# Four value buffers in a fused cross-attention, self-attention and expert kernel

## The chip, the cores and the metric

The kernel runs on one core of a Trainium2 chip, as one launch. The metric is the device time of the launch in microseconds (us); lower is better. A core has five engines that matter here: TensorE (PE in the profile; PEld is its weight load), VectorE (DVE), ScalarE (ACT), GpSimd (POOL) and SyncE (SP), which issues nearly all transfers.

## The reference

A batch of 64 sequences of 32 tokens, 256 wide, passes through three layers, each behind a layer norm and added back. The first attends from each sequence to its own 257 rows of context (`ctx_512`, 128 wide), the second attends within each sequence, with rotated queries and keys, the third sends each token to two of eight experts. Cut to that:

```
x = x + xattn(layernorm(x), ctx_512)     # 16 heads of 64; softmax over 257 context rows
x = x + attn(layernorm(x))               # 4 heads of 64; softmax over the 32 tokens of the sequence
x = x + ffn(layernorm(x))                # top 2 of 8 experts, silu(a) * b, 512 hidden
```

All of it is in float32.

## The kernel before, in words

The 2048 tokens are 16 tiles `t` of 128 tokens, each with four sequences `b`. The main loop goes over the 64 sequences `n` (`t, b`), and each iteration works at several tiles at once. `cross_probs` (L351 to L384) makes the scores of sequence n+1 against its context `kvT` (L364), the softmax on DVE and ACT, and the transposed weights `prT`. `cross_mix` (L395) runs in the odd iterations only: for the pair n-1 and n it multiplies the weights with the context itself, `kvA`, the "values" of a sequence. `cross_queries` prepares the queries of the next pair of tiles. The rest of a tile is a generator, `rest`: `cross_output` (values projected into `ov`, L429; output projection, L437), a norm `xns`, `self_attention`, a norm `xr`, and `route`, which picks two experts for each token and scatters the token's row into the table `routed` in DRAM (L616). Three tiles are at different steps of `rest`: "near", "far" and "late". A table of words, `steps`, says in which order an iteration takes these parts.

In `self_attention` the projected `qkv` is rotated on DVE, its queries and keys are turned by PE and copied by ACT into `qkT` (L471), PE multiplies them (L483), the softmax goes to a block-diagonal tile `diag` (L508), PE applies it (L513), ACT copies the result to `oT` (L520), and PE projects that (L527). A store of the tile (L530) follows on SP's queue.

The loads of the main loop are issued by SP, through `load` (L106): in iteration n the values of sequence n+2 (`load_values`, four transfers of 128 KB), the keys of sequence n+4, and at the end of a tile four small rows `u`. A buffer of `kvA` can be refilled once PE has mixed with it.

The expert layer works in blocks of 128 table rows that go to one expert. Six "early" blocks are formed while the last two tiles are not finished, their work interleaved with the rest of these tiles by the words of `do` (x: turn the block's rows, a and b: the two halves of the first layer, c: the second layer and the scatter into the output); the "late" blocks follow. For each block SP gathers the rows (`xg`, L733), and loads weights into "lanes" (L695). `prepared` (L763 to L777) turns the rows on PE, and DVE makes from the row's last columns the token's weight in this block (`gates` L773, `gate` L775) and its output row (`to` L777). These are used only in `combined` (L835 to L842). What the late blocks are is planned by some forty DVE operations once the last tile is routed (`late_blocks`, L656 to L945); SP reads its numbers (`meta_late`) before it gathers.

The order of instructions on PE and SP is that of the program text (`tc.manual_schedule(engines={SP, mybir.EngineType.PE})`). On DVE, ACT and POOL the framework's scheduler sets it when the kernel is built, by its own estimate of when each instruction could run; `tc.keep_in_program_order(...)` keeps one instruction of these engines behind the ones written ahead of it. Every engine runs its own instructions in the order so set. A tile's memory comes from a pool by tag: tiles of one tag share `bufs` buffers in turn, two in the pool `wk` unless the tile says otherwise.

Of the kernel before, what the change touches and what calls it, by code (L numbers as in the profile page):

```python
# [9 lines left out]
FP = mybir.dt.float32  # L10
U32 = mybir.dt.uint32
AF = mybir.ActivationFunctionType
ALU = mybir.AluOpType
# [3 lines left out]
P = 128  # L17
# [5 lines left out]
KVD = 128  # L23
M = 257
MC = 8
# [4 lines left out]
NE = 8  # L30
# [26 lines left out]
def block_kernel(  # L57
# [24 lines left out]
    nc = tc.nc  # L82
# [22 lines left out]
    def load(dst, src):  # L105
        nc.sync.dma_start(out=dst, in_=src)  # L106
# [10 lines left out]
    def pool(name, bufs):  # L117
        return ctx.enter_context(tc.tile_pool(name=name, bufs=bufs))

    kvp = pool("kv", 2)  # L120
# [10 lines left out]

    def load_values(n):

        kvA = kvp.tile([P, MC, KVD], FP, tag="kvA", bufs=3, name=f"kvA{n}")
        for h in range(4):
            load(kvA[h * SEQ : (h + 1) * SEQ, :, :], ctx_a[:, n, :, :])
        values.append(kvA)
# [15 lines left out]
    for n in range(2):  # L153
        load_values(n)
# [27 lines left out]
    wk = pool("wk", 2)  # L182
# [25 lines left out]
    for e in range(NE):  # L208
        tag, bufs, n = (("y", 4, D), ("bxT", 2, D), ("xg", 5, RW))[(e > 3) + (e > 5)]
# [10 lines left out]
    def bank(shape):  # L220
        return view(a_bank(), shape)
# [17 lines left out]
    def transposed(dst, src, n):  # L239

        pt = bank([n, P])
        for k in range(n):
            nc.tensor.transpose(pt[:, k, :], src[:, k * P : (k + 1) * P], ident)
        nc.scalar.copy(dst, pt)  # L244
# [200 lines left out]
    def self_attention(t, xn):  # L445
        xaT = wk.tile([P, 2, P], FP, tag="xaT", name=f"xaT{t}")
        transposed(xaT, xn, 2)
        yield
        qkv = wk.tile([P, 3 * D], FP, tag="qkv", name=f"qkv{t}")
        for lo, hi in ((0, 512), (512, 768)):  # L450
            pq = bank([hi - lo])
            for k in range(2):
                nc.tensor.matmul(  # L453
                    pq, xaT[:, k, :], awqkv_sb[:, k, lo:hi], start=(k == 0), stop=(k == 1)
                )
            nc.vector.tensor_tensor(qkv[:, lo:hi], pq, abqkv_bc[:, lo:hi], ALU.add)
        yield

        heads = qkv[:, : 2 * D].rearrange("p (h d) -> p h d", d=HD)
        x1, x2 = heads[:, :, 32:48], heads[:, :, 48:64]  # L460
        cb, sb = cos.to_broadcast([P, 2 * AH, 16]), sin.to_broadcast([P, 2 * AH, 16])
        x1s = wk.tile([P, 2 * AH, 16], FP, tag="x1s", name=f"x1s{t}")
        x2s = wk.tile([P, 2 * AH, 16], FP, tag="x2s", name=f"x2s{t}")
        tc.keep_in_program_order(nc.vector.tensor_tensor(x1s, x1, sb, ALU.mult))
        nc.vector.tensor_tensor(x2s, x2, sb, ALU.mult)
        nc.vector.tensor_tensor(x1, x1, cb, ALU.mult)
        nc.vector.tensor_tensor(x2, x2, cb, ALU.mult)
        nc.vector.tensor_tensor(x1, x1, x2s, ALU.subtract)
        nc.vector.tensor_tensor(x2, x2, x1s, ALU.add)
        yield  # L470
        qkT = wk.tile([P, 4, P], FP, tag="qkT", name=f"qkT{t}")  # L471
        transposed(qkT, qkv, 4)
        yield


        sc = wk.tile([P, 2, 2, SEQ], FP, tag="sc", name=f"sc{t}")
        mx = sm.tile([P, 2, 2, 1], FP, tag="amx", name=f"amx{t}")
        for par in range(2):
            pss = bank([2, SEQ])
            r = par * HD  # L480
            for hh in range(2):
                for b in range(4):
                    nc.tensor.matmul(  # L483
                        pss[b * SEQ : (b + 1) * SEQ, hh, :],
                        qkT[r : r + HD, hh, b * SEQ : (b + 1) * SEQ],
                        qkT[r : r + HD, 2 + hh, b * SEQ : (b + 1) * SEQ],
                        start=True,
                        stop=True,
                    )
            nc.vector.tensor_reduce(mx[:, par, :, :], pss, AX.X, ALU.max)  # L490
            nc.vector.tensor_tensor(
                sc[:, par, :, :],
                pss,
                mx[:, par, :, :].to_broadcast([P, 2, SEQ]),
                ALU.subtract,
            )
        scf = sc.rearrange("p a h s -> p (a h) s")
        pr = wk.tile([P, AH, SEQ], FP, tag="apr", name=f"apr{t}")
        nc.scalar.activation(pr, scf, AF.Exp, bias=zero, scale=QK_SCALE)
        sums = sm.tile([P, AH, 1], FP, tag="asums", name=f"asums{t}")  # L500
        nc.vector.tensor_reduce(sums, pr, AX.X, ALU.add)
        inv = sm.tile([P, AH, 1], FP, tag="ainv", name=f"ainv{t}")
        nc.vector.reciprocal(inv, sums)
        nc.vector.tensor_tensor(pr, pr, inv.to_broadcast([P, AH, SEQ]), ALU.mult)
        dg = diag[t % 2]
        for b in range(4):
            r = slice(b * SEQ, (b + 1) * SEQ)
            nc.vector.transpose(dg[r, :, r], pr[r, :, :])  # L508
        yield
        pot = bank([2, P])  # L510
        for h in range(AH):
            par, hh = h % 2, h // 2
            nc.tensor.matmul(  # L513
                pot[par * HD : (par + 1) * HD, hh, :],
                qkv[:, 2 * D + h * HD : 2 * D + (h + 1) * HD],
                dg[:, par * 2 + hh, :],
                start=True,
                stop=True,
            )
        oT = wk.tile([P, 2, P], FP, tag="oT", name=f"oT{t}")  # L520
        nc.scalar.copy(oT, pot)
        yield
        xb = wk.tile([P, D], FP, tag="xb", name=f"axb{t}")
        nc.gpsimd.tensor_tensor(xb, xs[t], abo_bc, ALU.add)
        po = bank([D])
        for k in range(2):
            nc.tensor.matmul(po, oT[:, k, :], awo_sb[:, k, :], start=(k == 0), stop=(k == 1))  # L527
        nc.vector.tensor_tensor(xs[t], po, xb, ALU.add)
        if t < NT - 2:
            nc.sync.dma_start(out=out[t * P : (t + 1) * P, :], in_=xs[t])  # L530
# [103 lines left out]
    def rest(t, cT, lastT, ut):  # L634

        yield from cross_output(t, cT, lastT, ut)
        xn = normed(t, "s")
        yield
        yield from self_attention(t, xn)
        xr = wk.tile([P, RW], FP, tag="xr", name=f"xr{t}")  # L640
        normed(t, "r", xr[:, 0:D])
        yield
        yield from route(t, xr)
# [66 lines left out]
    class Blocks:  # L710
# [44 lines left out]
        def prepared(self, b):  # L755

            xg, xw = self.xgs.pop(b)

            xT = xp.tile([P, 4, 2, SEQ], FP, tag="bxT", bufs=2, name=f"bxT_{self.name}{b}")
            if b < self.quarters:  # L760
                pt = bank([2, P])
                for k in range(2):
                    nc.tensor.transpose(pt[:, k, :], xg[:, k:D:2], ident)  # L763
                nc.scalar.copy(
                    xT.rearrange("p c k i -> p k c i"), pt.rearrange("p k (c i) -> p k c i", c=4)
                )
            else:
                nc.vector.transpose(
                    xT, xg[:, :D].rearrange("p (c j k) -> p c k j", c=4, k=2)
                )  # L770
            self.xTs[b] = xT
            gates = xp.tile([P, NE], FP, tag="gates", name=f"gates_{self.name}{b}")
            nc.vector.tensor_tensor(gates, xw[:, :NE], self.mine[:, b, :], ALU.mult)  # L773
            one = slice(b, b + 1)
            nc.vector.tensor_reduce(self.gate[:, one], gates, AX.X, ALU.add)  # L775
            if self.valid is None:
                nc.vector.tensor_copy(self.to[:, one], xw[:, NE:])  # L777
            else:
                nc.vector.scalar_tensor_tensor(
                    self.to[:, one], xw[:, NE:], self.valid[:, one],  # L780
                    self.spare[:, one], ALU.mult, ALU.add,
                )
# [354 lines left out]
    for n, (t, b) in enumerate(seqs):  # L1137
# [22 lines left out]
        if n + 2 < len(seqs):  # L1160
            load_values(n + 2)
# [177 lines left out]
```

## Time and profile before

| | us |
|---|---|
| median of 3 runs | 755.09 |
| lowest and highest run | 754.23, 756.03 |
| profiled execution: its own time | 758.28 |
| profiled execution: span, first to last instruction | 756.4 |
| busy in the span: PE, PEld, DVE, ACT, POOL | 723.9, 613.2, 508.4, 393.8, 322.2 |

The profile is of one execution, and its times within the span are counted from the span's start. A timeline line gives start, duration, engine, source line, operation, output and inputs, and in brackets how long the engine was idle before it and what released it. A line of waits gives who waited for whom, the total in us, how often, and the longest. A line of the form `L106 SPq` is SP's queue issuing a transfer: its duration is the issue, not the transfer. The attention tiles take about 66 us for each pair of tiles; the last tile's main loop ends near 533 us, the early blocks run to about 590 us, the late ones to 747 us.

### The profile page before, as it was taken

Reading aid. Unit: us, or ns where it says so; the run is one execution under the profiler, and the core shown is the slowest. Engines: PE = TensorE matmul, PEld = TensorE weight load, DVE = VectorE, ACT = ScalarE, POOL = GpSimd, SP = SyncE. Lnnn points to the kernel's source line nnn. Section 1 sums busy time; section 2 is a strip of 40 time slices with the busy share of each in tenths; the row PEclk is TensorE's granted clock in tenths of the full one; section 3 lists DMA queues with packets and bytes.
Section 4 is the critical chain, followed back from the end, with each engine's and each line's share of the span. In section 5 each row is a group of like instructions: output and inputs, shape, how many; then the busy total and the mean of one; then the engine's idle time right before and its main releaser. Section 6 shows DMA issues by size and latency. Waiting matters only on the chain.

```text
span 756.4 us, 22405 instructions
## 1 busy us (share of the span) xinstructions
PE 723.9 (96%) x8402; PEld 613.2 (81%) x8402; DVE 508.4 (67%) x1968; ACT 393.8 (52%) x1168; POOL 322.2 (43%) x598
## 2 busy tenths in 40 slices
PE   8799999999999999999999999999889999999993
PEld 7678888787788878778887877887679899998993
DVE  4758777777887777788777777887467434444442
ACT  3666666666666676666667666676242222221220
POOL 2101072846648385564838546421125213232332
PEclk9999999999999999999999999999999999999998
DMA  8784323433333344333334333253812994477431
GB/s 253 224 226 108 89 79 89 124 110 100 93 88 93 89 124 122 87 93 88 93 90 127 88 104 92 76 140 93 304 22 51 278 356 61 58 187 179 57 45 23
DMA packets 73087, 90.85 MB, mean 120 GB/s; under 512 B 24144, under 2 KB 56784, under 8 KB 72976
## 3 DMA queue, kind: packets, MB, share of 16 engines
q1 hardware_dynamic: 66448, 80.32, 37.8%
q0 software_dynamic: 6528, 9.06, 6.6%
q8 instruction: 68, 1.11, 0.6%
q14 instruction: 43, 0.35, 0.2%
HBM read 113.76 MB, written 13.16 MB: 168 GB/s over the span
## 4 chain that ended last, share of the span: by engine, by line
PE 66%; POOL 9%; DVE 8%; DMA 7%; issue 3%; SPq 2%; ACT 2%; POOLq 0%
PE psum L795 14%; PE psum L364 11%; PE psum L395 10%; PE psum L835 7%; PE psum L437 6%; PE psum L339 5%; POOL rprod L549 3%; POOL rprod L544 3%; PE psum L453 3%; PE psum L318 3%; PE psum L419 3%; SPq L106 2%; PE psum L527 1%; DVE prT L378 1%; POOL rpart L549 1%
## 5 line engine op out<-in xcount | busy, mean ns | idle before, releaser
L369 ACT ACTIVATE pr<-psum,nmx 128x257 f32<-128x257 f32 x256 | 120.4, 474 | 88.4 <-DVE nmx L368 86.8
L364 PE MATMUL psum<-kvT,q 128*128 128x257 f32 x512 | 141.3, 395 | 3.3 <-DMA kvT<-in_ctx_t 1.8
L395 PEld LDWEIGHTS psum<-prT,kvA 32*128 32x128 f32 x4096 | 119.3, 187 | 12.6 <-issue 5.6
L395 PE MATMUL psum<-prT,kvA 32*128 32x128 f32 x4096 | 126.7, 274 | 1.1 <-issue 0.4
L368 DVE TENSOR_REDUCE nmx<-psum 128x1 f32<-128x257 f32 x256 | 104.7, 414 | 32.6 <-PE psum L364 29.4
L376 ACT ACTIVATE pr<-pr,inv 128x256 f32<-128x256 f32 x256 | 114.7, 503 | 14.5 <-DVE inv L374 14.0
L364 PEld LDWEIGHTS psum<-kvT,q 128*128 128x128 f32 x512 | 88.7, 189 | 27.5 <-issue 7.5
L378 DVE STREAM_TRANSPOSE prT<-pr 128x512 f32<-128x512 f32 x128 | 89.9, 703 | 21.0 <-ACT pr L376 20.0
L842 POOL DMA_INDIRECT out_x<-y_late,to_late x28 | 43.4, 1550 | 104.1 <-DMA out_x<-y_late,to_late 25.1
L549 POOL TENSOR_TENSOR rprod<-rprod 128x128 f32<-128x128 f32 x192 | 75.4, 393 | 14.3
L544 POOL TENSOR_TENSOR rprod<-xr,wr_row 128x256 f32<-128x256 f32 x96 | 70.0, 729 | 7.5 <-DVE xr L236 0.8
L403 ACT COPY cT<-psum 128x512 f32<-128x512 f32 x64 | 34.2, 586 | 70.8 <-PE psum L395 67.5
L795 PE MATMUL psum<-bxT_late,lane 128*128 128x128 f32 x576 | 69.0, 275 | 0.0
L795 PEld LDWEIGHTS psum<-bxT_late,lane 128*128 128x128 f32 x576 | 68.0, 192 | 1.0
L437 PE MATMUL psum<-xwo_sb,ov 128*128 128x256 f32 x256 | 60.2, 382 | 1.6 <-DVE ov L429 1.3
L339 PE MATMUL psum<-xqT,xwq_sb 128*128 128x256 f32 x256 | 60.7, 381 | 0.5 <-ACT xqT L244 0.5
L437 PEld LDWEIGHTS psum<-xwo_sb,ov 128*128 128x128 f32 x256 | 48.0, 190 | 10.5 <-DVE ov L429 4.0
L339 PEld LDWEIGHTS psum<-xqT,xwq_sb 128*128 128x128 f32 x256 | 48.3, 190 | 8.0 <-ACT xqT L244 0.8
L817 ACT ACTIVATE sag_late<-psum,lane 128x128 f32<-128x128 f32 x72 | 20.5, 368 | 63.7 <-PE psum L795 55.3
L616 POOL DMA_INDIRECT routed<-xr,rslots x32 | 33.5, 1046 | 41.8 <-DMA routed<-xr,rslots 20.3
L369 ACT ACTIVATION_READ_ACCUMULATOR pr<-psum,nmx 128x1 f32 x256 | 51.1, 200 | 0.0
L411 POOL TENSOR_TENSOR xb<-x,xbo_bc 128x256 f32<-128x256 f32 x16 | 11.6, 729 | 85.5 <-DVE x L443 62.4
(268 smaller groups left out, 1195.9 us busy)
## 6 DMA issues: line engine op xcount, KB each, us to landing
kvA<-in_ctx_a SPq DMA_DIRECT2D x256, 128.0 KB
lane<-in_wall SPq DMA_DIRECT2D x24, 1028.0 KB
lane<-in_wall SPq DMA_DIRECT2D x24, 640.0 KB
lane2a<-in_wall SPq DMA_DIRECT2D x10, 1028.0 KB
kvT<-in_ctx_t SPq DMA_DIRECT2D x64, 128.5 KB
lane2b<-in_wall SPq DMA_DIRECT2D x10, 640.0 KB
xg_late<-routed SPq DMA_DIRECT2D x80, 32.0 KB
x<-in_x SPq DMA_DIRECT2D x16, 128.0 KB
```

The source lines that it names most:

```text
L339: nc.tensor.matmul(pq[:, mm, :], xwq_sb[:, k, m * P : (m + 1) * P], xqT[:, k, :], start=(k == 0), stop=(k == 1),)
L364: nc.tensor.matmul(s, qb[:, g * P : (g + 1) * P], kvT, start=True, stop=True)
L368: nc.vector.tensor_reduce(nmx, s, AX.X, ALU.max, negate=True)
L369: nc.scalar.activation(pr[:, g, :], s, AF.Exp, bias=nmx, accum_out=sums[:, g : g + 1])
L376: nc.scalar.mul(pr[:, i, :ML], pr[:, i, :ML], inv[:, i : i + 1])
L378: nc.vector.transpose(prT[:, :, two, :], pr[:, two, :ML].rearrange("p g (c m) -> p c g m", c=MC))
L395: nc.tensor.matmul(psum[:, at + h, i * P : (i + 1) * P], values[n][r, c, :], prT[r, c, :, :].rearrange("p g n -> p (g n)"), start=(c == 0) ...
L437: nc.tensor.matmul(po, ov[:, m, :], xwo_sb[:, m, :], start=False, stop=(m == XH // 2 - 1))
L544: nc.gpsimd.tensor_tensor(prod, xr[:, 0:D], wr_rows[i], ALU.mult)
L549: nc.gpsimd.tensor_tensor(dst, prod[:, :n], prod[:, n : 2 * n], ALU.add)
L795: nc.tensor.matmul(self.ps[b][half][:, j, :].rearrange("p (c i) -> p c i", c=4), w[:, lo : lo + P], self.xTs[b][:, :, k, :], start=(k == 0 ...
L835: nc.tensor.matmul(py, g[:, j * P : (j + 1) * P], layer[:, j, :], start=(j == 0), stop=(j == 3),)
```

## The change

The tag of the values gets a fourth buffer. The tags of `qkT` and `oT`, so far with two buffers, get one each. In `prepared`, the operation that makes `gates` and the one that makes `to` for the early blocks are kept in program order on DVE. The new buffer takes 4 KB of a partition, the two that go free 3 KB.

```diff
-        kvA = kvp.tile([P, MC, KVD], FP, tag="kvA", bufs=3, name=f"kvA{n}")
+        kvA = kvp.tile([P, MC, KVD], FP, tag="kvA", bufs=4, name=f"kvA{n}")
...
-        qkT = wk.tile([P, 4, P], FP, tag="qkT", name=f"qkT{t}")
+        qkT = wk.tile([P, 4, P], FP, tag="qkT", bufs=1, name=f"qkT{t}")
...
-        oT = wk.tile([P, 2, P], FP, tag="oT", name=f"oT{t}")
+        oT = wk.tile([P, 2, P], FP, tag="oT", bufs=1, name=f"oT{t}")
...
-            nc.vector.tensor_tensor(gates, xw[:, :NE], self.mine[:, b, :], ALU.mult)
+            tc.keep_in_program_order(
+                nc.vector.tensor_tensor(gates, xw[:, :NE], self.mine[:, b, :], ALU.mult)
+            )
...
-                nc.vector.tensor_copy(self.to[:, one], xw[:, NE:])
+                tc.keep_in_program_order(nc.vector.tensor_copy(self.to[:, one], xw[:, NE:]))
```

As built, PE, ACT, POOL and SP have the same instructions in the same order before and after. DVE has the same instructions; from the early blocks on, the `gates`, `gate` and `to` operations stand later in its order, with some shifts of the output operations among the plan's, and its load of the count of late blocks stands earlier. On SP the waits of the `kvA` loads name an earlier mix, and two further transfers have a wait for PE written out that a `kvA` wait ahead of them had covered.

## The prediction

> **What bounds the kernel now.** I read the stages first: the busy time of each engine by stretch. The columns are the stretch, its length, then busy us (and count) of PE, PEld, DVE, ACT and POOL, the granted clock, DMA share and GB/s.
>
> ```profile
> 396.00:463.00 67.00, 66.55 (x904) 54.09 (x900) 51.68 (x195) 42.68 (x126) 40.18 (x84) 1.00 0.35 94
> ...
> 525.00:560.00 35.00, 28.96 (x348) 22.84 (x349) 19.87 (x94) 12.97 (x33) 6.00 (x8) 1.00 0.54 181
> 560.00:592.00 32.00, 30.28 (x233) 28.27 (x233) 23.73 (x122) 9.90 (x29) 14.76 (x13) 1.00 0.29 58
> 592.00:640.00 48.00, 48.00 (x363) 46.01 (x362) 19.28 (x74) 12.50 (x42) 12.39 (x8) 1.00 0.86 257
> ```
>
> In the attention tiles (66 to 463 us) PE has work for 394.4 of 397 us, and so again from 592 us in the late expert blocks. Only the hand-over between them (525 to 592 us), where the last two tiles run beside the first six expert blocks, leaves PE idle, for 6.0 and 1.7 us. A change that leaves PE's work alone can gain there, and hardly elsewhere.
>
> Next the waits (us in total, times, longest), first SP's own:
>
> ```profile
> SPq L106 <- PE psum L395: 270.0, 29, 12.3
> ```
>
> SP spends 270 us waiting for a mix (L395) to free a values buffer. That looks like the target, but among PE's own waits the only one on an attention load is 1.8 us for kvT near 44 us; none is on kvA. SP's waiting is therefore free as long as nothing urgent stands behind it. So I looked at what does, in SP's timeline:
>
> ```profile
> 509.54 12.58 SPq L106 DMA_DIRECT2D kvA<-in_ctx_a  x8
> 522.21 1.47 SPq L530 DMA_DIRECT2D out_x<-x  x1
> ...
> 526.36 1.48 SPq L695 DMA_DIRECT2D lane<-in_wall  x2
> 528.45 3.90 SPq L733 DMA_DIRECT2D xg_early<-routed  x5
> ```
>
> The first kvA set of the first line leaves at 509.54, the second only at 520.41, after the first half of the mix of sequences 60 and 61. Behind it stand a store, the lanes' weights and the gathers of the first expert blocks. The engines' waits show who is late for these gathers, and DVE's timeline shows what stands behind each wait:
>
> ```profile
> DVE gates_early L773 <- DMA xg_early<-routed: 8.2, 4, 4.8
> ```
>
> The timeline:
>
> ```profile
> 534.31 0.17 DVE L773 TENSOR_TENSOR gates_early<-xg_early,mine_early 128x8 f32<-128x8 f32 x1 [2.27 <-DMA xg_early<-routed]
> ...
> 535.12 0.17 DVE L773 TENSOR_TENSOR gates_early<-xg_early,mine_early 128x8 f32<-128x8 f32 x1 [0.22 <-DMA xg_early<-routed]
> ...
> 536.57 0.17 DVE L773 TENSOR_TENSOR gates_early<-xg_early,mine_early 128x8 f32<-128x8 f32 x1 [0.95 <-DMA xg_early<-routed]
> ...
> 537.90 0.68 DVE L429 COPY ov<-psum 128x512 f32<-128x512 f32 x1
> ...
> 549.71 0.17 DVE L773 TENSOR_TENSOR gates_early<-xg_early,mine_early 128x8 f32<-128x8 f32 x1 [4.75 <-DMA xg_early<-routed]
> ...
> 550.89 0.41 DVE L236 TENSOR_SCALAR xns<-x,mvs,rstds 128x256 f32<-128x256 f32 x1 [0.68 <-POOL rstds L233]
> ```
>
> The number in brackets is idle time. DVE takes its instructions in order; gates that need a gathered block stand ahead of tile 15's `ov` copy (whose first input is ready near 535.75) and of its normalisation `xns`. PE pays for that:
>
> ```profile
> 534.34 0.51 PE L763 MATMUL psum<-ident,xg_early 128*128 128x128 f32 x2 [0.62 <-DMA xg_early<-routed]
> ...
> 538.64 1.99 PE L437 MATMUL psum<-xwo_sb,ov 128*128 128x256 f32 x8 [1.27 <-DVE ov L429]
> ...
> 544.55 0.66 PE L513 MATMUL psum<-diag,qkv 128*64 128x128 f32 x8 [1.68 <-DVE diag L508]
> ...
> 551.36 0.44 PE L243 MATMUL psum<-ident,xns 128*128 128x128 f32 x2 [1.06 <-DVE xns L236]
> ```
>
> **What the Trainium skill says.** "DMA: Bandwidth & Descriptors", section "Anatomy of one DMA", says that DMA engines do not wait on semaphores: the wait is served on the issuing sequencer before dispatch. The trace agrees: nothing behind the second kvA set left SP before 520.41. "DVE: scalar operands, raw-bit mode, write accounting and state across instructions", section "Flops that outlive an instruction", calls the DVE's queue one in-order queue; the `ov` copy behind the gates shows it. On the fourth buffer itself no price is needed.
>
> **The change, part by part.** In the built program PE, ACT, POOL and SP issue the same instructions in the same order as before, and the waits of PE, ACT and POOL are the same. So the single buffers of `qkT` and `oT` add no wait: tile t's copy already waits for its own matmuls, which PE runs after the last reader of tile t-1's. I price them at nothing.
>
> *Fourth values buffer.* Sequence n+2's values now take the buffer of n-2 and not of n-1. For odd n that removes the wait for half of the mix of iteration n. In the attention tiles this ends a wait that PE never felt: 0, with 0.5 us either way for small shifts. At the start the set was issued at 41.29, right behind the kvT issue of 40.84, so it waited for SP alone: 0. At the end sequence 63's set needs only the mix finished near 506.2. The store L530 then sets SP's pace; its input (DVE L528) is ready at 518.79. Store 0.4, four u issues 1.83 (to 521.1), then 0.8 to the lane weights (521.9), and as before 2.1 us from there to the first gather: 524.0 in place of 528.45, some 4.4 us sooner. Landing moves from about 534.2 to about 529.8, ahead of PE's use at 533.7. PE's 0.62 goes. The 5.0 MB of lanes (three of 1028 and 640 KB), which ran at 350 to 390 GB/s from 529 to 544, run from about 524.6 to 539.6; each lane is read later than that.
>
> *Pinned gates.* Block 0's three operations move between tile 13's slot sums, those of blocks 1 and 2 behind tile 14's `xr`, block 3's behind tile 15's diagonal, block 4's into the last routing, block 5's behind the late plan. The 2.27 + 0.22 + 0.95 and the 4.75 us of DVE idle time go. With tile 13's slot arithmetic no longer waiting (its PE input is ready at 533.2), tile 15's `ov` starts as soon as its matmuls end. PE's 1.27 goes. What is late next is tile 14's diagonal: from the scores' end (about 540.95) to L513 is 3.6 us of DVE and ACT work against 2 us of PE work, whatever came before, so the 1.68 stays. Tile 15's statistics start at 544.52 and need some 1.5 us to `xns`, PE asks at 550.30: without the 4.75 the 1.06 goes.
> Sum on PE up to tile 15's query product: 0.62 + 1.27 + 1.06 = 2.95 us sooner.
>
> *What is given back.* Block 3's gates (three operations, 0.45 us from first to last with their dependences) now stand ahead of block 1's `sag` product (L822), which PE meets with 0.3 us to spare: 0.1 to 0.2. Block 4's stand in the chain from the last routing to the late plan, which sets the gather that PE waits for at 590.88 (1.12 us of idle time). Counted instruction by instruction at DVE's issue step of 0.1 us, that chain is 0.3 to 0.5 longer: 0.4. Block 5's come after the plan's numbers that SP needs: 0. The late blocks' reordered gates and DVE's load of the block count, 0.55 us long at 745.9, fall into DVE idle times of 1.0 to 2.6 us: 0, and at most 0.4 gained where the last scatter started 1.1 us after its input against 0.7 before.
>
> Net: 2.95 - 0.15 - 0.4 = 2.4 us. The profiled execution has a span of 756.4 and a time of 758.28; its equal after would be 754.0 and 755.9. It lies 3.2 us above the median of the three runs (755.09), so I take the sum from the median: **752.7 us**. About 0.2%, 1.5 us, is what a measurement here can tell from no change.
>
> **Rivals.**
> *Given back at the late plan.* The gather at 590.88 hangs on a chain: route of tile 15, POOL's 1.68 us power, 8 us of the plan on DVE, SP, 3.3 us of landing. If it moves by only half of PE's 2.95, or the moved gates delay it by 1.5 in place of 0.4, PE meets it with 2 to 3 us of idle time, and 0.5 to 1.4 us remain: about 754.1, within 0.2%. Against it: every link starts from a PE or DVE instruction that moves too.
> *Slower: the weights' burst moved under the mix.* Now the full DMA window starts at 529, when PE's last mix (529.05) has its instructions; moved to 524.6 it lies over 256 more of PE's instructions. "Runtime: NRT & Kernel Launch", section "Instruction fetch mechanics", says instructions come in by DMA in blocks of 16 KiB, 256 instructions, mostly hidden; the page's instruction queue moved 68 packets and 1.11 MB, which agrees in size. A scatter in the full window took up to 4.8 us to land against a median of 2.7, so a fetch could be 2.1 us late. One late fetch, fully felt, leaves a gain of 0.3; from the second on the change is slower: 4.2 - 2.4 gives about 756.9. Against it: the last mix ran in 3.85 us inside the full window, as others do outside it.
> *The values were late after all.* If the attention tiles held hidden waits for kvA, up to the 2.6 us of PE idle time there would come on top: 750.1. Against it: no PE wait names kvA.
> *The change does nothing of it*: if PE's three idle times come back from another releaser (ACT's second half of `ov`, ready within 0.1 us of need, is the nearest), the time stays at 755.
>
> **How the numbers follow.** Main case with its give-back, 0.68 (752.0 to 753.5); late-values case 0.05: faster together 0.73. Given back at the plan or nothing of it, 0.18: same. Burst 0.09: slower. The range 750.6 to 755.6 takes the main case, part of the deep one and nearly all of "same".
>
> **What would show it.** After: the first early gather issued near 524 and landed near 530; no kvA wait of 9 us on SP near 511 to 520; no DVE idle time ahead of gates; PE idle times of 0.62, 1.27 and 1.06 gone, 1.68 kept; the late gather met with 1.2 to 1.7 us; 66 us for two tiles as before. The forecast is wrong if the attention tiles change by over 0.5 us, if the 1.68 goes too, or if the late gather does not come some 2.5 us sooner.

## The result and the profile after

The changed kernel takes 752.98 us (median of 20 runs, 750.66 to 759.04) against 756.73 us for the kernel before in the same comparison (20 runs, 753.72 to 759.81). The ratio is 0.9957, with a 95% interval of 0.9938 to 0.9976: faster, by 1.8 to 4.7 us. In the later comparisons the median of the kernel before lay at 756.6 to 757.1 as well, above the 755.09 of its first three runs. A second set of 12 runs of the changed kernel had a median of 752.55, ratio 0.9939 (0.9917 to 0.9962). The profiled execution after has a span of 749.4 us and a time of 751.2.

The busy time of the first hand-over stretch, columns as before:

```profile
525.00:560.00 35.00, 32.15 (x385) 27.76 (x378) 21.21 (x99) 13.50 (x30) 9.32 (x12) 1.00 0.39 126
```

PE is idle for 2.85 us of this stretch where it was 6.04. The stretch holds slightly different work in the two profiles, so I don't count with it; the sums below use starts of the same PE instructions.

SP's own waits after (total, times, longest):

```profile
SPq L530 <- DVE x L528: 152.5, 13, 13.5
SPq L106 <- PE psum L395: 103.3, 28, 7.8
```

SP still waits, but 152.5 us of it now stand ahead of the store L530, on DVE's `x`. The wait for a mix has fallen from 270.0 to 103.3, so most of SP's waiting has moved and not gone. SP's timeline at the hand-over:

```profile
514.13 0.36 SPq L530 DMA_DIRECT2D out_x<-x  x1
514.53 1.82 SPq L106 DMA_DIRECT2D u<-u_last  x4
517.16 1.48 SPq L695 DMA_DIRECT2D lane<-in_wall  x2
519.25 3.87 SPq L733 DMA_DIRECT2D xg_early<-routed  x5
```

The last mix starts at 524.19 here and at 529.05 before. The first early gather therefore leaves SP 4.94 us ahead of the last mix, against 0.60 us before: 4.3 us sooner. DVE's timeline (the `gates` are L774 here, L773 before):

```profile
528.69 0.16 DVE L774 TENSOR_TENSOR gates_early<-xg_early,mine_early 128x8 f32<-128x8 f32 x1
...
530.38 0.69 DVE L429 COPY ov<-psum 128x512 f32<-128x512 f32 x1 [1.20 <-PE psum L419]
...
543.30 0.16 DVE L774 TENSOR_TENSOR gates_early<-xg_early,mine_early 128x8 f32<-128x8 f32 x1
```

No `gates` line has a bracket any more; `ov` waits for PE and not behind a gather. The last mix on PE, and PE's waits from there to the late gathers:

```profile
524.19 3.85 PE L395 MATMUL psum<-prT,kvA 32*128 32x128 f32 x128
...
537.47 0.66 PE L513 MATMUL psum<-diag,qkv 128*64 128x128 f32 x8 [1.68 <-DVE diag L508]
544.02 2.85 PE L453 MATMUL psum<-awqkv_sb,xaT 128*128 128x512 f32 x8 [0.57 <-ACT xaT L244]
549.79 0.39 PE L483 MATMUL psum<-qkT 64*32 64x32 f32 x32 [0.46 <-ACT qkT L244]
564.45 0.61 PE L561 MATMUL psum<-wr_sb,xrT 128*128 128x8 f32 x4 [0.52 <-ACT xrT L244]
581.75 0.51 PE L763 MATMUL psum<-ident,xg_late 128*128 128x128 f32 x2 [0.49 <-DMA xg_late<-routed]
```

The 0.62 (gathered rows), 1.27 (`ov`) and 1.06 (`xns`) are gone; the 1.68 for the diagonal is still there. The same points in the kernel before:

```profile
529.05 3.85 PE L395 MATMUL psum<-prT,kvA 32*128 32x128 f32 x128
...
552.26 2.85 PE L453 MATMUL psum<-awqkv_sb,xaT 128*128 128x512 f32 x8 [0.46 <-ACT xaT L244]
...
590.88 0.51 PE L763 MATMUL psum<-ident,xg_late 128*128 128x128 f32 x2 [1.12 <-DMA xg_late<-routed]
```

From the last mix to tile 15's query product (L453) PE took 23.21 us before and takes 19.83 now; to the L763 that waits for a late gather, 61.83 and 57.56.

One thing in this pair of profiles was not forecast: the last mix starts 4.86 us earlier, before the hand-over has begun. Was that the change, or one execution? The first experiments ask it together with the question which part of the change does what.

### The profile page after: what moved, and what is told of

Read it like the earlier page. It is cut to its first block, busy times and chain, and to the rows that moved or that the text cites. A ratio compares the mean times of both kernels' runs of the same rounds, so it can differ in the third digit from the quotient of the medians.

```text
span 749.4 us, 22405 instructions
## 1 busy us (share of the span) xinstructions
PE 720.8 (96%) x8402; PEld 612.4 (82%) x8402; DVE 508.5 (68%) x1968; ACT 393.5 (53%) x1168; POOL 322.0 (43%) x598
## 4 chain that ended last, share of the span: by engine, by line
PE 70%; DMA 8%; DVE 7%; POOL 7%; SPq 3%; ACT 2%; issue 2%; POOLq 0%; DVEq 0%; ACTq 0%
PE psum L797 14%; PE psum L364 11%; PE psum L395 11%; PE psum L437 6%; PE psum L837 6%; PE psum L339 5%; PE psum L453 4%; PE psum L318 3%; PE psum L419 3%; POOL rprod L549 3%; POOL rprod L544 2%; SPq L106 2%; DMA kvA<-in_ctx_a 2%; PE psum L527 2%; PE psum L243 1%
## 5 line engine op out<-in xcount | busy, mean ns | idle before, releaser
L395 PE MATMUL psum<-prT,kvA 32*128 32x128 f32 x4096 | 124.3, 273 | 0.5 <-ACT pr L369 0.4
L437 PE MATMUL psum<-xwo_sb,ov 128*128 128x256 f32 x256 | 60.1, 382 | 0.3
L437 PEld LDWEIGHTS psum<-xwo_sb,ov 128*128 128x128 f32 x256 | 48.0, 190 | 8.9 <-DVE ov L429 2.3
L616 POOL DMA_INDIRECT routed<-xr,rslots x32 | 33.4, 1043 | 43.7 <-DMA routed<-xr,rslots 23.2
```

Source lines behind the costliest of these rows:

```text
L395: nc.tensor.matmul(psum[:, at + h, i * P : (i + 1) * P], values[n][r, c, :], prT[r, c, :, :].rearrange("p g n -> p (g n)"), start=(c == 0) ...
L437: nc.tensor.matmul(po, ov[:, m, :], xwo_sb[:, m, :], start=False, stop=(m == XH // 2 - 1))
```

## The experiments

Every kernel was timed beside the kernel before on the same chip. PE, ACT, POOL and SP have the order of the changed kernel in all of them, except SP's values loads in `ahead3` and the last two, which move work on PE; a few copies on ACT follow these moves, and in `three_moves` one operation of POOL. Each gave one profile; the table puts what is read from it in one place. "Gather" is how long before the last mix SP issued the first early gather. "Product" and "late" are the times on PE from the start of the last mix to tile 15's first query product (L453) and to the use of the second late gather (the L763 with the idle time; the first late gather is turned just ahead of it, almost without a wait; the expectations call this point the first late gather's use). "Chain" is the time from the last of the last route's four matmuls (L561) to SP's issue of the first late gather. All are differences of two starts.

| kernel | values buffers, gates | gather | product | late | chain | median us, ratio to before (95%) |
|---|---|---|---|---|---|---|
| before (page above) | 3, ahead of ov and xns | 0.60 | 23.21 | 61.83 | 13.33 | 755.09 alone |
| `before_again` | same | 0.83 | 22.97 | 61.18 | 13.34 | 755.81, 0.9991 (0.9966 to 1.0016) |
| `single_only` | same | 0.82 | 23.18 | 61.19 | 13.32 | 756.95, 1.0002 (0.9976 to 1.0029) |
| `front3` | 3, 0 to 4 ahead of ov | 0.77 | 21.18 | 59.20 | 13.30 | 754.78, 0.9971 (0.9947 to 0.9995) |
| `pins_only` | 3, pinned | 0.83 | 20.33 | 58.69 | 13.35 | 754.11, 0.9952 (0.9933 to 0.9972) |
| `front4` | 4, 0 to 4 ahead of ov | 5.05 | 19.83 | 57.50 | 13.31 | 753.95, 0.9965 (0.9949 to 0.9980) |
| changed | 4, pinned | 4.94 | 19.83 | 57.56 | 13.35 | 752.98, 0.9957 (0.9938 to 0.9976) |
| `after_again` | 4, pinned | 4.62 | 19.83 | 58.01 | 13.38 | 752.55, 0.9939 (0.9917 to 0.9962) |
| `ahead3` | 4, pinned | 5.02 | 19.83 | 58.11 | 13.42 | 752.12, 0.9943 (0.9918 to 0.9967) |
| `fourth_only` | 4, not pinned | 16.18 | 19.83 | 58.10 | 13.35 | 763.08, 1.0070 (1.0044 to 1.0096) |
| `a0_first` | 4, pinned, PE's work moved | 5.04 | 18.15 | 56.39 | 13.36 | 751.18, 0.9920 (0.9893 to 0.9948) |
| `three_moves` | 4, pinned, PE's work moved | 4.97 | 17.42 | 56.59 | 13.33 | 752.46, 0.9929 (0.9904 to 0.9954) |

The runs of one kernel spread over some 5 to 10 us, so medians separate only the larger steps; the hand-over columns repeat within 0.3 us ("product") and 0.7 us ("late", which has a gather's landing in it), and carry the argument.

**Was the earlier last mix an accident?** The kernel before once more:

> The kernel before once more, for a second profile. Theory G: mixes 12, 16, 20, 24 and 28 at 4.3 to 4.5 us again, 479 to 480 us from mix 1 to the last mix. Theory B: 3.8 us, 475 to 476 us; then the hand-over alone separates the two kernels, 59.5 to 62 us from the last mix to the first late gather's use against 56.6 to 58.1 in the changed one.

One mix, PE's timeline of the kernel before, and then the same mix in its second profile:

```profile
489.98 4.41 PE L395 MATMUL psum<-prT,kvA 32*128 32x128 f32 x128
```

```profile
488.12 3.85 PE L395 MATMUL psum<-prT,kvA 32*128 32x128 f32 x128
```

The mixes 12, 16, 20, 24 and 28 (counted from 0) took 4.33 to 4.46 us in the first profile, from start to the instruction that follows. In the second they took 3.78 to 3.79, and the way from mix 1 to the last mix fell from 479.58 to 475.84 us. That is theory B; the execution of the first profile, at 758.28 us, also lies 3.2 us above the median of 755.09. The changed kernel has 475.30, so over the attention tiles the two kernels are 0.5 us apart, and the profiles of the other kernels lie as close together (475.3 to 476.0), `fourth_only` aside, whose last mix is late for a reason of its own.

The theory that the changed buffers had ended those stalls (with three buffers each second set is refilled in the middle of a mix) was tried by itself:

```diff
-        if n + 2 < len(seqs):
-            load_values(n + 2)
+        for v in range(n + 2 + (n > 16), min(n + 3 + (n >= 16), len(seqs))):
+            load_values(v)
```

> The changed kernel, except that from iteration 16 on the values of sequence n+3 and not of n+2 are loaded in iteration n: with four buffers each second set waits again for the first half of the mix of its own iteration, as before, and its transfers start in the middle of that mix. PE, DVE, ACT and POOL have the same order as in the changed kernel; the end of SP's queue is a set shorter. Theory A (a refill that starts inside a mix stalls PE there): mixes 12, 16, 20, 24 and 28 take 4.3 to 4.5 us, the last mix starts 2 to 3.5 us later than in the changed kernel, the hand-over is the same: 2 to 3.5 us slower than the changed kernel, no gain on before larger than 2 us. Theory B (accident of one execution): all mixes 3.8 us, within 0.2% of the changed kernel.

Theory A fell: with the refill back in the middle of the mixes, these five took 3.78 to 3.82 us, 476.01 us from mix 1 to the last, and the time is that of the changed kernel. `pins_only`, below, has three buffers and the same SP waits as before, and its mixes take 3.78 us too.

The changed kernel once more:

> The changed kernel once more, for a second profile. Theory A: no mix over 3.9 us again; last mix within 1 us of 524.2 us; the hand-over from the last mix to the first late gather 57 to 58 us. Theory B (accident): one or more of the mixes 12 to 28 at 4.3 us or more. The ratio to before should be 0.994 to 0.998.

All the named mixes took 3.78 us. The last mix came later than expected (526.96 us, since mix 1 started at 51.02 and not at 48.89); 475.94 us lie between. So everything ahead of the last mix is out of the comparison, and what remains is the hand-over: 61.83, 61.18 and 61.19 us with the old order and buffers, 57.56, 58.01 and 58.11 with the new (the third from `ahead3`). The means, 61.40 and 57.89, differ by **3.5 us**. It isn't a matter of how fast the gathers landed: the issue of the first late gather by SP follows the last mix by 57.3 to 57.7 us in the first three profiles and by 54.0 in the other three, 3.5 us again.

**Single buffers alone.**

```diff
-        qkT = wk.tile([P, 4, P], FP, tag="qkT", name=f"qkT{t}")
+        qkT = wk.tile([P, 4, P], FP, tag="qkT", bufs=1, name=f"qkT{t}")
-        oT = wk.tile([P, 2, P], FP, tag="oT", name=f"oT{t}")
+        oT = wk.tile([P, 2, P], FP, tag="oT", bufs=1, name=f"oT{t}")
```

> The kernel before with single buffers for qkT and oT and nothing else: orders and waits of all engines are those of the kernel before, only places in memory differ. As forecast these buffers are worth nothing: within 0.2% of before. Theory G (the long mixes 12, 16, 20, 24 and 28 come from the program of the kernel before, not from one execution): they take 4.3 to 4.5 us here too, the last mix starts 479 to 480 us after mix 1. Theory B (accident of one execution): they take 3.8 us, 475 to 476 us.

Ratio 1.0002, hand-over 61.19 us, mixes of 3.78 us: nothing, as forecast. They are what the fourth values buffer is paid with.

**Pins alone, buffer alone.** `pins_only` is the changed kernel with `bufs=3` and without the two single buffers:

```diff
-        kvA = kvp.tile([P, MC, KVD], FP, tag="kvA", bufs=4, name=f"kvA{n}")
+        kvA = kvp.tile([P, MC, KVD], FP, tag="kvA", bufs=3, name=f"kvA{n}")
```

> Three values buffers and two each for qkT and oT, as before; only the two pinned operations. DVE's order is then that of the changed kernel, SP's order and waits are those of the kernel before. Theory A (the hand-over gains what the forecast says, the fourth buffer also ends stalls of PE inside the mixes): mixes 12, 16, 20, 24 and 28 take 4.3 to 4.5 us again, against 3.8 in the others; the first early gather leaves SP 0.5 to 0.7 us ahead of the last mix; PE's idle times of 1.27 (for ov) and 1.06 (for xns) are gone, the 0.62 for the gathered rows stays; 1.5 to 2.3 us gained less 0.4 given back: 1 to 2 us faster than before. Theory B (the long mixes of the kernel before were the accident of one execution): all mixes take 3.8 us here too; the hand-over as in A, the time 1 to 2 us below before. Theory C (the pins bring all of it): as fast as the changed kernel, 3 us below before.

PE's and DVE's timelines at the first gather:

```profile
529.37 0.50 PE L763 MATMUL psum<-ident,xg_early 128*128 128x128 f32 x2 [0.45 <-DMA xg_early<-routed]
```

```profile
529.34 0.17 DVE L774 TENSOR_TENSOR gates_early<-xg_early,mine_early 128x8 f32<-128x8 f32 x1 [0.51 <-DMA xg_early<-routed]
530.94 0.69 DVE L429 COPY ov<-psum 128x512 f32<-128x512 f32 x1 [1.10 <-PE psum L419]
```

The gather is as late as before, PE and DVE both wait half a microsecond for it, but `ov` no longer stands behind it. The product comes 20.33 us after the last mix, 2.8 us sooner than before (23.12, the mean of three), and only 0.50 later than in the changed kernel. So in the hand-over the pins account for 2.8 us and the buffer, given the pins, for 0.5. The long mixes that theory A expected didn't come, which is theory B's side of the table. The gain is more than the 1 to 2 us expected. In the medians `pins_only` lies 1.1 and 1.6 us above the two sets of the changed kernel, but the intervals overlap, and its ratio, 0.9952, lies between theirs. Timing alone therefore doesn't rule out theory C, that the pins bring all of it; against it stand the profiles, by the 0.5 us.

`fourth_only` keeps the buffers and drops the pins:

```diff
-            tc.keep_in_program_order(
+            (
                 nc.vector.tensor_tensor(gates, xw[:, :NE], self.mine[:, b, :], ALU.mult)
             )
...
-                tc.keep_in_program_order(nc.vector.tensor_copy(self.to[:, one], xw[:, NE:]))
+                nc.vector.tensor_copy(self.to[:, one], xw[:, NE:])
```

> Four values buffers and single qkT and oT, without the two pins. SP's order and waits are those of the changed kernel. DVE's order differs from before in one place: the scheduler puts the gates of the first four early blocks between tile 14's xr and the first score maximum of sequence 63, 15 us of DVE's order earlier than before, and the fifth two maxima later. Theory A: DVE stands still there from about 517 us until the fourth gather has landed, near 525; the maxima, the softmax and with it the last mix come late; 4 to 8 us are lost to the changed kernel, 1 to 5 us to the kernel before. Theory C' (the buffer brings it all, the pins nothing): as fast as the changed kernel, 3 us below before.

DVE's timeline, then PE's:

```profile
518.25 0.41 DVE L236 TENSOR_SCALAR xr<-x,mvr,rstdr 128x256 f32<-128x256 f32 x1 [0.66 <-POOL rstdr L233]
...
526.72 0.17 DVE L774 TENSOR_TENSOR gates_early<-xg_early,mine_early 128x8 f32<-128x8 f32 x1 [8.06 <-DMA xg_early<-routed]
```

```profile
530.85 1.02 PE L561 MATMUL psum<-wr_sb,xrT 128*128 128x8 f32 x4 [9.71 <-ACT xrT L244]
```

The gates stand right behind tile 13's `xr` at 518.25 (the expectation calls it tile 14's, by mistake), and the first gather leaves SP only at 520.88. DVE stands still for 8.06 us with the score maxima of sequence 63 behind it, PE for 9.71, and the last mix starts at 537.06. Theory A, but its size was too small: 10.1 us lost to the changed kernel (763.08 against 752.98) and some 6 to the kernel before (3.3 to 7.3 by the interval), where 4 to 8 and 1 to 5 were expected. I had counted to the gathers' landing; the likely remainder, not measured by itself, is what DVE and ACT have to catch up with afterwards. After the late mix the hand-over is that of the changed kernel. So the pins are no decoration: with four buffers and no pins the framework's scheduler puts the gates where they hold up the softmax.

**Two remedies for one wait.** If the late gather and the gates ahead of `ov` make the idle time only together, either remedy should do. Two kernels put the gates of blocks 0 to 4 back ahead of `ov`, pinned there; the second has three buffers:

```diff
             self.xTs[b] = xT
+            if b >= 5 or self.valid is not None:
+                self.weighed(b, xw)
+
+        def weighed(self, b, xw):
             gates = xp.tile([P, NE], FP, tag="gates", name=f"gates_{self.name}{b}")
...
+            if unit == "g":
+                for b in range(5):
+                    blocks.weighed(b, blocks.xgs[b][1])
-            if unit in work:
+            elif unit in work:
...
-    do("far x0 near near far near far a0 far x2 x1 b0 near near near c0 near far near x3 far")
+    do("g far x0 near near far near far a0 far x2 x1 b0 near near near c0 near far near x3 far")
```

> The changed kernel with the gates, gate and to of blocks 0 to 4 moved forward on DVE: all fifteen operations, pinned, behind tile 14's slot sums and ahead of tile 15's ov copy, close to where they stood before; block 5's stay behind the late plan. Four values buffers; PE, ACT, POOL and SP as in the changed kernel. Theory D (a gather that is late and gates that stand ahead of ov make the idle times together, so either remedy does): all five gathers have landed by then, DVE doesn't wait, 20 us from the last mix to tile 15's query product as in the changed kernel (19.8 there, 23.2 before), the time within 0.2% of it. Theory E (the order alone decides): PE's 1.27 for ov comes back, 21 us or more, 1 to 3 us slower than the changed kernel. If the forecast's give-back in the chain of the late plan was real, the late gather comes 0.3 to 0.5 us sooner here.

> The same order of DVE as in the run with the gates moved forward, but three values buffers and two each for qkT and oT, so SP's waits are those of the kernel before. Theory D: DVE waits 3 to 4 us for the first gathers again, PE has its 0.6 for the gathered rows and its 1.27 for ov; the 1.06 for xns, which came from block 5's gates, is absent; 22.0 to 22.3 us from the last mix to tile 15's query product; 2 to 2.5 us slower than with four buffers. Theory F (the pins work by block 5 alone): 21 us or less.

With four buffers: 19.83 us, the same as the changed kernel to the hundredth, with the gates in almost the old place. With three, PE's timeline:

```profile
529.45 0.51 PE L763 MATMUL psum<-ident,xg_early 128*128 128x128 f32 x2 [0.52 <-DMA xg_early<-routed]
533.00 1.99 PE L437 MATMUL psum<-xwo_sb,ov 128*128 128x256 f32 x8 [0.52 <-DVE ov L429]
538.91 0.66 PE L513 MATMUL psum<-diag,qkv 128*64 128x128 f32 x8 [1.68 <-DVE diag L508]
```

Both waits are back, and 1.35 us with them (21.18 against 19.83): theory D in kind. The size is short of the 2.2 us or more that I expected, because here most of tile 13's slot arithmetic (tile 14's in the expectation, by mistake) stands ahead of the gates and not, as before, between them and `ov`. DVE's own wait for the first gather falls from 2.27 to 0.57 us, and PE's for `ov` from 1.27 to 0.52. The wait for `xns` (1.06) is absent, since block 5's gates stand behind the late plan here. In the medians `front3` is 0.8 us above `front4`, inside the intervals, so the 2 us or more that I expected of the time was not there.

`front4` also takes block 4's gates out of the chain from the last route to the late plan. The chain is 13.31 us there, 13.33 to 13.42 in the kernels that have them in it, and 13.30 to 13.35 in the others that don't (the three with the old order, `front3` and `fourth_only`).

**The wait that stays.** The forecast left the 1.68 us for the diagonal, because PE has too little work beside it. `a0_first` gives it more:

```diff
-    do("far x0 near near far near far a0 far x2 x1 b0 near near near c0 near far near x3 far")
+    do("far x0 near near far near a0 far x2 x1 far b0 near near near c0 near far near x3 far")
```

> The changed kernel with one move in the order of PE's work: block 0's first half (16 matmuls of L797, 2.05 us), until now behind the wait for tile 14's diagonal, goes ahead of L513, and blocks 1 and 2 are turned ahead of L527 instead of behind it. The forecast said that the 1.68 us wait for the diagonal stands because 3.6 us of DVE and ACT work have only 2 us of PE work beside them. If so, the 2.05 us cover it: L513 starts about 0.4 us later than before the move with no idle time, PE stands perhaps 0.2 us for oT, and the hand-over from the last mix to tile 15's query product falls from 19.8 to 18.2 to 18.8 us; if the late gather comes as much sooner, the time is 1 to 1.6 us below the changed kernel's, 0.5 to 0.7% below before. Rival: the lane's weights or DVE's chain for xns set the end instead, and PE waits there for 1 us or more: no gain on the changed kernel.

The first waits of PE behind the last mix (525.84) are then

```profile
543.99 2.85 PE L453 MATMUL psum<-awqkv_sb,xaT 128*128 128x512 f32 x8 [0.57 <-ACT xaT L244]
549.76 0.39 PE L483 MATMUL psum<-qkT 64*32 64x32 f32 x32 [0.46 <-ACT qkT L244]
```

The wait for the diagonal is gone, the product comes 1.68 us sooner and the late gather is used 1.5 us sooner (56.39 against 57.89). The median is 751.18, ratio 0.9920 (0.9893 to 0.9948): about 1.4 to 1.8 us below the changed kernel's two medians, taken in another comparison, so the profile carries that difference more than the timing does. It is the lowest median of all, though its interval overlaps those of the changed kernel.

`three_moves` covers two of the remaining waits as well:

```diff
-    do("far x0 near near far near far a0 far x2 x1 b0 near near near c0 near far near x3 far")
+    do("far x0 near near far near a0 far x2 x1 far near b0 near near c0 near far x3 near far")
```

> As the run with block 0's first half moved, and two more moves on PE: block 0's second half goes behind the turn of tile 15's xns, in place of the 0.57 us wait for ACT's copy xaT, and block 3 is turned ahead of the scores L483, in place of the 0.46 us wait for qkT. If each wait is covered: 17.8 to 18.4 us from the last mix to the query product plus 1.95 us for the half that now lies between, so 19.6 to 20.3 us, and the late gather's use 2 to 2.6 us sooner after the last mix than in the changed kernel (57.6 to 58.1 there): 55.2 to 56 us; time 2 to 2.6 us below the changed kernel. Rival: ACT, which now does block 0's activations ahead of oT and takes table loads of 1.28 us between them, becomes late: gain below 1 us or none.

The product comes at 17.42 us (I had added 1.95 for a half that already lay ahead of the product, so the figure to compare is 17.8 to 18.4), the 0.57 is gone and the 0.46 is 0.22. But the late gather is used 56.59 us after the mix, no sooner than with one move. PE's timeline shows a wait that was not there:

```profile
563.75 0.44 PE L243 MATMUL psum<-ident,xr 128*128 128x128 f32 x2 [0.75 <-DVE xr L236]
```

Tile 15's normalisation `xr` takes the 0.7 us back. DVE's timeline names what it waits for, and POOL's what stands ahead of that:

```profile
563.28 0.41 DVE L236 TENSOR_SCALAR xr<-x,mvr,rstdr 128x256 f32<-128x256 f32 x1 [2.52 <-POOL rstdr L233]
```

```profile
561.63 0.99 POOL L616 DMA_INDIRECT routed<-xr,rslots  x1 [0.30 <-issue]
562.65 0.59 POOL L233 TENSOR_TENSOR rstdr<-ver,minus_half 128x1 f32<-128x1 f32 x1
```

DVE has `ver`, the input of `rstdr`, ready at 560.75. But the moves on PE have also changed the scheduler's order on POOL in one place: the second of tile 14's scatters into `routed` (L616) now stands ahead of `rstdr`. In `a0_first`, as in the changed kernel, it stands behind it, and `xr` waits 1.45 us and not 2.52. The rival named ACT; it was POOL. Pinning `rstdr` ahead of the scatter would test this, which no run here does.

## Why the prediction was right, and where its sum was off

The forecast was a gain of 2.4 us in the hand-over; the hand-over gained 3.5. That the forecast time, 752.7 us, came within 0.3 us of the measured 752.98 is in part luck: it was counted from the median of three runs, 755.09, and the median of 20 is 1.6 us higher. The low start and the small gain cancel. By its own steps:

- **Attention tiles, 0 with 0.5 us either way:** held. 475.30 and 475.94 us from mix 1 to the last mix against 475.84 and 475.42 (`before_again`, `single_only`). The 4.3 us in the first pair of profiles belong to one execution. In these tiles SP's waiting for a mix was free.
- **First gather 4.4 us sooner:** 4.3 in the profiled pair. The store L530 sets SP's pace, as worked out.
- **PE's 0.62 goes, by the buffer:** held; given the pins it is worth 0.50, the difference of `pins_only` and the changed kernel (the second profile of the kernel before has 0.34 in its place).
- **1.27 and 1.06 go, 1.68 stays:** held, and the sum 2.95 was small. Taking starts instead of the idle times in brackets, the profiled pair gained 3.38 to the product (3.29 by the means of three). L437 came 1.44 us nearer to the matmuls that precede it and not 1.27, the turn of `xns` 1.22 nearer and not 1.06. The Trainium skill, "Perfetto Trace Analysis", section "Summary: the profiler window per engine type", says that of a TensorE instruction the start is recorded and the end estimated; the two extra pieces of 0.16 to 0.17 us agree with that. In the changed kernel, where L437 doesn't wait, it starts 0.53 us after the L433 ahead of it, whose recorded duration is 0.70: 0.17 us before its recorded end. A bracket counts only from that end. No run here measures the ends themselves. A further 0.24 came just behind the product, at the next L243, whose waits of 0.10 us went.
- **Given back, 0.15 and 0.4:** this step failed. The chain from the last route to the late gather's issue is 13.33 to 13.42 us with block 4's gates in it and 13.30 to 13.35 without: some 0.04 us, not 0.4. I had counted each instruction at DVE's issue step; the likely reason, not tried by itself, is that in a chain of dependences they fall into gaps. Block 3's gates cost nothing that shows: from product to last route PE takes 20.78 us after, against 21.0 to 21.1 before. The second late gather met PE with 0.49, 1.02 and 1.08 us against 1.12, 0.75 and 0.59, not the forecast 1.2 to 1.7: it is the landing that varies (2.7 to 3.4 us from its own issue to its use over all profiles), not the chain.
- **The rivals:** the late plan gave nothing back, as the issue of its first gather came 3.5 us sooner, all of PE's gain. ACT's half of `ov` didn't take the wait over: PE has no wait for `ov` left. The late weights' burst under the mix didn't show; the last mix took 3.78 us in every profile with the gathers 5 us sooner. (The landing of 4.8 us that priced it is that of a scatter at 505.2 us: from 505 to 510 us the DMA engines moved 172 GB/s, from 529 to 544, the full window, 372.) Hidden waits for the values would have shortened the attention tiles, which didn't happen.

2.95 plus some 0.35 in such pieces, 0.24 behind the product and no give-back is 3.5. The timed ratios, 0.9957 and 0.9939, say 1.8 to 6.3 us over their intervals and agree with it.

What I had not seen is the part that explains why the two edits come together: not that both take away waits (the pins alone would have taken 2.8 of the 3.3 us to the product) but that the buffer without the pins costs 6 us.

## What to carry to other kernels

A long wait on a queue is worth what stands behind it at the moment when another engine is short of work: of SP's 270 us of waiting only the 4.3 us ahead of the early gathers mattered, and with the pins in place these were worth half a microsecond. A wait that arises from a late transfer and an in-order queue together can be taken away at either end, and the second remedy adds only the remainder; but when a buffer changes what a scheduler believes of arrival times, look at where it moves the readers of that data. Before explaining a difference between two profiles, take a second one of each: here 4.3 us of the first pair were one execution's.

## What the runs showed of the hardware

Of eleven new profiles none repeated the five long mixes of the first (4.33 to 4.46 us against 3.78, the weight loads of mix 28, for one, idle for 0.24 us in its middle with "issue" and no releaser named); what held them is open. Mixes 7, 11, 15, 19 and 23 seem to repeat in every profile, before or after, with 4.14 to 4.52 us from their start to the instruction that follows, but these are not slow mixes: from their first matmul to the start of their last they take 3.58 us like the others, where the five took 4.13 to 4.26. The rest is a wait of the next instruction for DVE, here of the changed kernel behind mix 15:

```profile
277.81 0.63 PE L243 MATMUL psum<-ident,qkv 128*128 128x128 f32 x4 [0.31 <-DVE p_last L384]
```

It is 0.29 to 0.67 us long in the twelve profiles, at every eighth iteration, with three buffers and with four. A stall inside a run of matmuls and a wait behind it look alike when one counts from start to next start.

The end of the kernel is a lottery of some microseconds: from PE's last matmul to the end of the span the profiles show 10.5 to 16.9 us, where POOL's last scatters into the output follow one another. In the worst of them, `pins_only`, POOL's last two were each held for another's landing:

```profile
740.73 1.55 POOL L844 DMA_INDIRECT out_x<-y_late,to_late  x1 [4.03 <-DMA out_x<-y_late,to_late]
745.26 1.55 POOL L844 DMA_INDIRECT out_x<-y_late,to_late  x1 [2.98 <-DMA out_x<-y_late,to_late]
```
